# A Fourier stage: row 64 sent earlier, the last inverse matrices in two transfers, the last unit pipelined

## The chip, the cores and the metric

The kernel runs on one core of a Trainium2 chip. The metric is the device time of one execution in microseconds (us). The engines are named as in the profile: PE is the matrix engine (PEld its weight loads), DVE the vector engine, ACT the scalar engine, POOL the general engine, SP the engine that only issues transfers here.

## The reference, cut to what matters

A network of four layers over `x` (4, 96, 64, 64): a state-space layer, a depthwise convolution with a small MLP, linear attention with a quantized MLP, and a Fourier layer with a quantized MLP. The change is in the Fourier layer, which works on `t` (4 batches, 4096 tokens, 96 channels):

```python
h = jnp.einsum('bnc,hc->bnh', _ln_t(t), w1)                # 192 hidden channels
h = relu(bn1(h))
X = jnp.fft.fft(h, axis=1, norm='ortho')                   # over the 4096 tokens
xr = relu(X.real * rd - X.imag * idg + rb)
xi = relu(X.imag * rd + X.real * idg + ib)
y = jnp.fft.ifft(xr + 1j * xi, axis=1, norm='ortho').real
t = t + bn2(jnp.einsum('bnh,ch->bnc', y, w2))
```

## The kernel before

The layers run one after the other, the first to about 2610 us, the convolution to 3010, the attention with its MLP to 3319, the Fourier layer to 3863, the last MLP (`qffn`) to the end. All data of the Fourier layer stay on the chip, in `t` and `h`.

The transform of 4096 tokens is split as 128 x 32. A *unit* is half of the hidden channels (96) of one batch, so there are 8 units. A unit's forward transform goes in four *groups* of 24 of its channels (6 blocks of 4): `its` lists the 32 pairs of unit and group. One turn of the loop over `j`, called a slot below, carries several groups at different stages (matmuls are counted as the trace shows them, each of the code's fp32 ones as two):

- `over_n1(j)` (L1138): 12 matmuls with the 128-point matrix on the tile `hh`, then on DVE the twiddle products (L1142), on POOL two sums (L1150)
- `over_n2(j - 1)` (L1159 to L1162): the 32-point transform; DVE multiplies the imaginary part (L1165), ACT scales the real part in 12 instructions (L1174), POOL forms sum and difference (L1177, L1178)
- `fold(j - 2)`: ACT relu (L1184), DVE relu and add into `zz` and into `z64`, the row at frequency 64 (L1189, L1192), ACT negates one part (L1195)
- `over_k2(j - 3)` (L1207, L1208): 24 matmuls of the inverse 32-point transform, copied by ACT into the tile `bt` of the unit (L1209)
- `row64(u)` in slot 4u + 7: four small matmuls on `z64` (L1217), an ACT copy to `r` (L1219), a transfer `d<-r` to DRAM (L1221), and a transfer `bt<-d` back into row 64 of `bt` (L1222). The second waits on SP for the first
- in slots 4u + 8 to 4u + 11, two blocks a slot of the inverse 128-point transform of unit u: `over_k1` fetches four inverse matrices, 256 KB, into `gt` (L1226, two buffers), runs four matrices' matmuls on `bt` (L1229) and has ACT copy the result to `ys` (L1231). `w2` then projects (L1237), and DVE adds the result to `t` (L1241 for one half, L1243 for the other). All 32 rows `n` of `idft` take eight blocks, and every unit reads the same ones

Beside these, the next batch is normalized (`norm1`, `norm2`, L1104 to L1115) and multiplied by `w1` (L1124, L1126) in the slots of units 0 to 5, so that slots there take about 14.7 to 14.9 us, and those of units 6 and 7 about 11.6 us. After slot 31 nothing new is begun; slots 36 to 39 hold the blocks of unit 7 alone, and slots 40 to 43 are empty.

The order on PE, DVE, ACT and POOL is the order in which the code is written (`manual_schedule`). SP is not among these; the framework orders its transfers. PSUM has eight banks: two for `m` (`misc`, used by `norm1`, `norm2`, `w1`, `row64`, `over_k1` and `w2`), two for `s1`, one each for `xr` and `xi`, two for `i1` (`over_k2`). The tile `hh` has three buffers of 12 KB a partition; units 6 and 7 take the last new ones in slot 20.

Of the kernel before, what the change touches and what calls it, by code (L numbers as in the profile page):

```python
# [9 lines left out]
F32 = mybir.dt.float32  # L10
# [8 lines left out]
B, C, HW, L = 4, 96, 64, 4096  # L19
# [7 lines left out]
N1, N2, NF = 128, 32, 192  # L27
# [23 lines left out]
class Net:  # L51
# [1031 lines left out]
    def fourier(self, dram, t, h):  # L1083
        tc, nc, ins = self.tc, self.nc, self.ins
        CG, G, K1 = 24, 6, 65
        PER = CG // G
        units = [(b, half) for b in range(B) for half in range(2)]
        its = [(u, g) for u in range(len(units)) for g in range(0, CG, G)]
        with ExitStack() as ctx:
            wk = ctx.enter_context(tc.tile_pool(name="fw", bufs=1))  # L1090
            pln = ctx.enter_context(tc.tile_pool(name="fp", bufs=1, space=PSUM))
            self.tc.keep_in_program_order(nc.scalar.preload_act_table_set(ACT_EXP_LN))
            nbs, bc, bs = (self.dft2[:, k * 128 : (k + 1) * 128] for k in range(3))
            hh, bt, z64, f, x, av, zz = {}, {}, {}, {}, {}, {}, {}
            ft = [t[:, b * L : (b + 1) * L].rearrange("p (a n) -> p n a", n=N2) for b in range(B)]

            def misc(rows):
                return pln.tile([128, MB], F32, name="m_ps", tag="m", bufs=2)[:rows]
# [10 lines left out]
            def norm2(a, kept):  # L1109
                ps = misc(C)  # L1110
                nc.tensor.matmul(ps, self.ones, kept.pop(a), start=True, stop=True)
                rs = wk.tile([C, MB], F32, name="ln_rs", tag="rs")
                nc.scalar.activation(rs, ps, AF.Ln, scale=1.0 / C, bias=self.eps[:C])
                nc.scalar.activation(rs, rs, AF.Exp, scale=-0.5)
                nc.gpsimd.tensor_mul(h[:C, a : a + MB], h[:C, a : a + MB], rs)  # L1115
# [16 lines left out]
            def over_n1(i):  # L1132

                u, g = its[i]
                ps = pln.tile([128, 2, MB], F32, name="s1_ps", tag="s1")
                for d in range(G):
                    a = d % 3 * 2 * K1
                    nc.tensor.matmul(ps[:, d // 3, a : a + 2 * K1], hh[u][:, g + d], self.dft1, start=True, stop=True)  # L1138
                pp = []
                for k in range(2):  # L1140
                    p = wk.tile([128, G, 2, K1], F32, name=f"p{k}", tag=f"p{k}")
                    nc.vector.tensor_mul(  # L1142
                        p.rearrange("p (a g) r k -> p a g (r k)", a=2),
                        ps[:, :, : 6 * K1].rearrange("p a (g k) -> p a g k", g=3),
                        self.twid[:, k : k + 1, None, :].to_broadcast([128, 2, 3, 2 * K1]),
                    )
                    pp.append(p)
                f[i] = wk.tile([128, 2, G, K1], F32, name="f", tag="f", bufs=2)
                for r in range(2):
                    nc.gpsimd.tensor_add(f[i][:, r], pp[0][:, :, r, :], pp[1][:, :, 1 - r, :])  # L1150
# [46 lines left out]
            def over_k2(i):  # L1197

                u, g = its[i]
                z = zz.pop(i)  # L1200
                if g == 0:
                    bt[u] = wk.tile([N1, N2, C], F32, name="bt", tag="bt", bufs=2)
                for e in range(0, G, 3):
                    ps = pln.tile([N1, 3, 128], F32, name="i1_ps", tag="i1", bufs=2)
                    for d in range(3):
                        zd = z[:, e + d].rearrange("p k m -> p (k m)")
                        nc.tensor.matmul(ps[:, d], zd[:, 64:], bc, start=True, stop=False)  # L1207
                        nc.tensor.matmul(ps[:, d], zd[:, :128], bs, start=False, stop=True)  # L1208
                    nc.scalar.copy(  # L1209
                        bt[u].rearrange("p n (g c) -> p g n c", c=4)[:, g + e : g + e + 3],  # L1210
                        ps.rearrange("p g (n c) -> p g n c", c=4),
                    )

            def row64(u):
                ps = misc(CG)[:, :128]
                for k in range(2):
                    nc.tensor.matmul(ps, z64[u][:, k], self.dft64[:, k], start=k == 0, stop=k == 1)  # L1217
                r = wk.tile([CG, N2, 4], F32, name="r64", tag="r64", bufs=2)
                nc.scalar.copy(r, ps.rearrange("p (n c) -> p n c", c=4))  # L1219
                d = dram.tile([1, N2 * C], F32, name="d64", tag="d64", bufs=2)  # L1220
                nc.sync.dma_start(d.rearrange("o (n g c) -> g (o n) c", n=N2, c=4), r)  # L1221
                nc.sync.dma_start(bt[u][64:65].rearrange("p n c -> p (n c)"), d)  # L1222

            def over_k1(u, n, kept):
                gt = wk.tile([N1, 4, N1], F32, name="gt", tag="gt", bufs=2)
                nc.sync.dma_start(gt, ins["idft"][:, n : n + 4])  # L1226
                ps = misc(C).rearrange("p (n a) -> p n a", n=4)
                for d in range(4):
                    nc.tensor.matmul(ps[:, d], bt[u][:, n + d], gt[:, d], start=True, stop=True)  # L1229
                kept[u, n] = wk.tile([C, MB], F32, name="ys", tag="ys", bufs=2)  # L1230
                nc.scalar.copy(kept[u, n], ps.rearrange("p n a -> p (n a)"))  # L1231

            def w2(u, n, kept):

                b, half = units[u]
                ps = misc(C)
                nc.tensor.matmul(ps, self.a_w2[:, half, :], kept.pop((u, n)), start=True, stop=True)  # L1237
                ps = ps.rearrange("p (n a) -> p n a", n=4)
                td = ft[b][:, n : n + 4]
                if half == 0:  # L1240
                    nc.vector.scalar_tensor_tensor(td, ps, self.b2, td, ALU.add, ALU.add)  # L1241
                else:
                    nc.vector.tensor_add(td, td, ps)  # L1243

            engines = {mybir.EngineType.PE, mybir.EngineType.DVE, mybir.EngineType.Activation, mybir.EngineType.Pool}
            with tc.manual_schedule(engines=engines):
                for n in range(0, N2, 2):
                    w1(0, n)
                kept, sq = {}, {}
                for j in range(len(its) + 12):  # L1250
                    ub, k = divmod(j - 2 * PER, PER)
                    blocks = [(ub, n) for n in (8 * k, 8 * k + 4)] if 0 <= ub < len(units) else []

                    u, k = divmod(j, PER)
                    b = u // 2 + 1
                    normed = b < B and u % 2 == 0
                    tokens = list(range(8 * k, 8 * k + 8, 2)) if b < B and u % 2 else []
                    a = 2 * k * MB

                    def turn(count):  # L1260
                        for _ in range(min(count, len(tokens))):
                            w1(b, tokens.pop(0))

                    if j < len(its):
                        over_n1(j)

                    if normed:
                        norm1(b, a, sq)
                    if k:
                        turn(2)  # L1270
                    if 2 <= j < len(its) + 2:
                        fold(j - 2)
                    if blocks:
                        over_k1(*blocks[0], kept)
                    if normed and k:
                        norm2(a - MB, sq)
                    if 1 <= j < len(its) + 1:
                        over_n2(j - 1)
                    if normed:
                        norm1(b, a + MB, sq)  # L1280
                    if blocks:
                        w2(*blocks[0], kept)
                        over_k1(*blocks[1], kept)
                    if not k:
                        turn(2)
                    if 3 <= j < len(its) + 3:
                        over_k2(j - 3)
                    if normed:
                        norm2(a, sq)
                    if (j - 7) % PER == 0 and 0 <= (j - 7) // PER < len(units):  # L1290
                        row64((j - 7) // PER)
                    turn(len(tokens))
                    if blocks:
                        w2(*blocks[1], kept)
                    if normed and k == PER - 1:
                        norm2(a + MB, sq)


def build(tc, ins, out):
# [155 lines left out]
```

## Time and profile before

| What | us |
|---|---|
| median of three runs | 4002.08 (3991.09 to 4005.25) |
| the profiled execution | 4009.92 |
| its span | 4007.80 |
| of it the Fourier stage, 3319 to 3863 | 544 |
| PE, ACT, DVE, POOL busy in that stage | 471, 296, 242, 214 |
| the stretch of unit 7's blocks, 3836 to 3863: PE, DVE, ACT busy | 20.3, 8.8, 5.9 of 27 |

Over the whole span PE is busy 3303.4 us and DVE 3186.9, most of it in the first layer, which the change does not touch. The mean granted PE clock is 0.855 of full speed over the span, 0.94 in the Fourier stage and 0.80 in the stretch of unit 7. In the lines of a timeline the columns are the start, the length, the engine, the source line, the operation, what it writes and reads, the count, and in brackets how long the engine had been idle before and what ended that. In a window's row they are the span of time, its length, busy time and count of PE, PEld, DVE, ACT and POOL, the granted PE clock, the DMA share and GB/s.

### The profile page before, as it was taken

To read this page: it belongs to the slowest core of one execution; us is meant where nothing else is said; L and a number is where in the kernel's file an instruction comes from. 1 tells how busy PE (TensorE), PEld (TensorE's weight loads), DVE (VectorE), ACT (ScalarE), POOL (GpSimd) and SP (SyncE) were. 2 spreads that over 40 slices of the span, in tenths; PEclk is the share of its full clock that TensorE was granted. 3 is DMA by queue.
4 is the path that set the end of the run, shared out by engine and by line. 5 is a ranking of instruction groups with operands and counts; after the bars stand their busy time and mean duration, and the time that the engine had idled before them with its cause. 6 is when DMAs were issued, how large, how long until landed. Compare 5 with 4: busy or idle time off the path is not lost. (4 is left out here: it accounts for less than half of the span.)

```text
span 4007.8 us, 45514 instructions
## 1 busy us (share of the span) xinstructions
PE 3303.4 (82%) x14174; PEld 1425.1 (36%) x14174; DVE 3186.9 (80%) x2772; ACT 2421.0 (60%) x4644; POOL 2944.4 (73%) x1571
## 2 busy tenths in 40 slices
PE   6888878888888788888878888686999888998877
PEld 3222222222222222222222222186445435676642
DVE  5999999999999999999999999832652593444549
ACT  4666667667666766766666666231445575665547
POOL 2999999999999999999999999811000273444428
PEclk8888878878888888888888888667999998999989
DMA  7567566756666675666567666375000000011111
GB/s 184 137 161 174 135 160 157 175 131 168 166 154 148 162 170 138 162 166 167 141 161 169 147 155 158 82 226 178 1 0 1 1 0 6 25 35 35 42 41 54
DMA packets 183295, 468.13 MB, mean 117 GB/s; under 512 B 53240, under 2 KB 55170, under 8 KB 179972
## 3 DMA queue, kind: packets, MB, share of 16 engines
q1 hardware_dynamic: 183048, 465.21, 46.8%
q8 instruction: 113, 1.85, 0.2%
q14 instruction: 134, 1.07, 0.1%
HBM read 391.53 MB, written 73.50 MB: 116 GB/s over the span
## 5 line engine op out<-in xcount | busy, mean ns | idle before, releaser
L496 POOL TENSOR_TENSOR hs<-hs,crep 128x1024 f32<-128x1024 f32 x768 | 1796.2, 2363 | 27.2 <-DVE hs L490 22.4
L454 PE MATMUL rep<-dbl,sel_b 32*128 32x512 f32 x1152 | 409.0, 787 | 460.4 <-DVE hs L490 434.4
L474 POOL TENSOR_TENSOR up<-udb,brep 128x1024 f32<-128x1024 f32 x256 | 604.9, 2363 | 8.5 <-DMA brep<-cd 8.5
L468 ACT ACTIVATE da<-ddb,nega 128x1024 f32<-128x1024 f32 x512 | 584.9, 1149 | 14.9 <-DMA ddb<-dd 7.4
L468 ACT ACTIVATE dap<-ddb,nega 128x1024 f32<-128x1024 f32 x256 | 286.3, 1118 | 419.6 <-DVE hs L490 417.5
L515 PE MATMUL y<-hs,sel_r 128*32 128x512 f32 x3072 | 483.2, 697 | 6.1 <-POOL hs L496 6.1
L490 DVE TENSOR_TENSOR_SCAN hs<-da,state,rep 128x1024 f32<-128x1024 f32 x192 | 450.8, 2348 | 16.7
L490 DVE TENSOR_TENSOR_SCAN hs<-da,state,u 128x1024 f32<-128x1024 f32 x192 | 450.9, 2348 | 11.2 <-DVE u L486 1.4
L490 DVE TENSOR_TENSOR_SCAN hs<-dap,state,up 128x1024 f32<-128x1024 f32 x192 | 447.1, 2329 | 7.0 <-ACT dap L468 6.9
L454 PEld LDWEIGHTS rep<-dbl,sel_b 32*128 32x128 f32 x1152 | 109.6, 219 | 761.6 <-issue 510.0
L210 PE MATMUL ps<-n,w_x 97*64 97x512 f32 x1536 | 368.0, 622 | 8.1 <-ACT n L323 5.4
L486 DVE TENSOR_TENSOR u<-udb,rep 128x1024 f32<-128x1024 f32 x256 | 314.6, 1229 | 42.1 <-PE rep L454 10.9
L486 DVE TENSOR_TENSOR rep<-udb,rep 128x1024 f32<-128x1024 f32 x256 | 310.7, 1214 | 0.4
L1038 POOL CAST hq<-y 128x512 fp8e5<-128x512 f16 x192 | 118.0, 638 | 229.3 <-issue 143.0
L210 PEld LDWEIGHTS ps<-n,w_x 97*64 97x64 f32 x1536 | 109.8, 141 | 258.8 <-issue 209.2
L515 PEld LDWEIGHTS y<-hs,sel_r 128*32 128x32 f32 x3072 | 66.6, 117 | 364.5 <-issue 192.7
L382 POOL TENSOR_TENSOR du<-delta,xc 128x512 f32<-128x512 f32 x96 | 122.3, 1274 | 67.5 <-DMA gp_x<-in_x 52.1
L1177 POOL TENSOR_TENSOR av<-av,ec 128x780 f32<-128x780 f32 x32 | 58.8, 1838 | 152.3 <-ACT av L1174 152.3
L224 PE MATMUL ps<-xc,xproj 64*102 64x512 f32 x384 | 163.2, 1014 | 3.5 <-ACT xc L344 3.5
L358 ACT COPY dbl<-ps 102x512 f32<-102x512 f32 x64 | 34.3, 588 | 210.4 <-PE ps L224 210.4
L911 POOL MEMSET h<- 1x4096 f32 x1 | 3.5, 3506 | 212.9 <-DVE n L824 212.9
L490 DVE TENSOR_TENSOR_SCAN hs<-da,rep 128x1024 f32<-128x1024 f32 x64 | 146.5, 2289 | 5.4
(256 smaller groups left out, 6545.7 us busy)
## 6 DMA issues: line engine op xcount, KB each, us to landing
ddb<-dd SPq DMA_DIRECT2D x768, 128.0 KB
udb<-ud SPq DMA_DIRECT2D x768, 128.0 KB
crep<-cd SPq DMA_DIRECT2D x512, 128.0 KB
brep<-cd SPq DMA_DIRECT2D x256, 128.0 KB
dd<-delta SPq DMA_DIRECT2D x64, 384.0 KB
ud<-du SPq DMA_DIRECT2D x192, 128.0 KB
band<-in_band SPq DMA_DIRECT2D x24, 1024.0 KB
gt<-in_idft SPq DMA_DIRECT2D x64, 256.0 KB
```

The costliest lines, as they stand in the source:

```text
L210: nc.tensor.matmul(ps[rows], w[:, 64 * p : 64 * p + 64], rhs[:, at.start + shift : at.stop + shift], start=k == 0, stop=k == len(ws) - 1, ...
L224: nc.tensor.matmul(ps, w[rows, p], x[rows, p], start=start and p == 0, stop=p == 2)
L382: nc.gpsimd.tensor_mul(u, m["delta"][:, of], m["xc"][:, of])
L454: nc.tensor.matmul(x[:, at], sel_b[rows, order[t][1]], made[k]["dbl"][rows, at], start=True, stop=True)
L468: nc.scalar.activation(da, made[k]["dd", h, j], AF.Exp, scale=nega[:, col : col + 1])
L474: nc.gpsimd.tensor_mul(u, made[k]["ud", h, j], made[k]["brep", g])
L486: nc.vector.tensor_mul(u, made[k]["ud", h, j], x)
L490: nc.vector.tensor_tensor_scan(hs[:, 1:], made[k].pop(("da", t)), u, 0.0 if s == 0 else st, ALU.mult, ALU.add)
L496: nc.gpsimd.tensor_mul(hs[:, :T], hs[:, 1:], made[k]["crep", order[t][1]])
L515: nc.tensor.matmul(made[k]["y", p][row : row + 32], sel_r, made[k]["hs", t][:, at], start=False, stop=True, skip_group_check=True,)
L1038: nc.gpsimd.tensor_copy(q[:, m, :], y2, saturate=False)
L1177: nc.gpsimd.tensor_add(v[:, 2:4], v[:, 0:2], ec)
```

## The change

Four things change, all in `fourier`.

- `fetch(k)` loads half of `idft` (16 of 32 matrices, 1 MB) into a free buffer of the tag `hh`, in slots 25 and 29. From then on `over_k1` takes its matrices from there if it finds its `n` in `late`, and else fetches `gt` as before. So `gt` is still used by units 0 to 3 and in six blocks of unit 4.
- The loop ends after slot 35. Unit 7's eight blocks follow in a loop of their own, in which `over_k1` of a block is issued ahead of `w2` of the block before.
- `w2` of unit 7 writes to the two banks of `i1` in place of `m`; for that the tile of `i1` becomes 4 x 128 wide, of which `over_k2` uses three quarters.
- `row64(u)` is issued in slot 4u + 6 in place of 4u + 7.

```diff
@@ over_k2
-                    ps = pln.tile([N1, 3, 128], F32, name="i1_ps", tag="i1", bufs=2)
+                    ps = pln.tile([N1, 4, 128], F32, name="i1_ps", tag="i1", bufs=2)[:, :3]
@@ ahead of over_k1
+            late = {}
+
+            def fetch(k):
+
+                g = wk.tile([N1, CG, N2, 4], F32, name="hh", tag="hh", bufs=3)
+                g = g.rearrange("p g n c -> p (g n c)")[:, : N2 // 2 * N1].rearrange("p (n a) -> p n a", n=N2 // 2)
+                nc.sync.dma_start(g, ins["idft"][:, k * N2 // 2 : (k + 1) * N2 // 2])
+                for n in range(0, N2 // 2, 4):
+                    late[k * N2 // 2 + n] = g[:, n : n + 4]
+
             def over_k1(u, n, kept):
-                gt = wk.tile([N1, 4, N1], F32, name="gt", tag="gt", bufs=2)
-                nc.sync.dma_start(gt, ins["idft"][:, n : n + 4])
+                if n in late:
+                    gt = late[n]
+                else:
+                    gt = wk.tile([N1, 4, N1], F32, name="gt", tag="gt", bufs=2)
+                    nc.sync.dma_start(gt, ins["idft"][:, n : n + 4])
@@ w2
-                ps = misc(C)
+                if u < len(units) - 1:
+                    ps = misc(C)
+                else:
+                    ps = pln.tile([N1, 4, 128], F32, name="i1_ps", tag="i1", bufs=2)[:C].rearrange("p n a -> p (n a)")
@@ the loop over slots
-                for j in range(len(its) + 12):
+                for j in range(len(its) + 4):
...
                     if j < len(its):
                         over_n1(j)
+                    if j in (len(its) - 7, len(its) - 3):
+                        fetch((j - len(its) + 7) // 4)
...
-                    if (j - 7) % PER == 0 and 0 <= (j - 7) // PER < len(units):
-                        row64((j - 7) // PER)
+                    if (j - 6) % PER == 0 and 0 <= (j - 6) // PER < len(units):
+                        row64((j - 6) // PER)
...
+                last = [(len(units) - 1, n) for n in range(0, N2, 4)]
+                for k, block in enumerate(last):
+                    over_k1(*block, kept)
+                    if k:
+                        w2(*last[k - 1], kept)
+                w2(*last[-1], kept)
```

## The prediction

> **What bounds the kernel now.** The page first: VectorE is busy 80% and TensorE 82% of the span, but by stages. The windows view of 3319 to 3863 us, the Fourier stage, gives PE 471 of 544 us, ACT 296, DVE 242, POOL 214: PE leads there, and short holes in PE are what an edit can win. So I read the waits of 3420 to 3862 next ("who <- whom: us in total, times, longest"):
>
> ```profile
> PE m_ps L1237 <- ACT ys L1231: 23.3, 23, 4.5
> PE m_ps L1229 <- DMA bt<-d: 16.6, 5, 5.6
> PE m_ps L1229 <- issue: 8.3, 2, 4.8
> SPq L1222 <- DMA d<-r: 25.2, 8, 3.8
> ```
>
> Together 24.9 us of PE stood before the first `over_k1` of seven units, waiting for row 64; no line names PE waiting for `gt<-in_idft`. Then the timeline (start, length, engine, line; in brackets the idle time before) at one unit's boundary, SP, PE and ACT:
>
> ```profile
> 3786.49 0.33 SPq L1221 DMA_DIRECT2D d<-r  x1
> 3788.31 0.85 ACT L1184 ACTIVATE av<-av 128x780 f32<-128x780 f32 x1 [1.84 <-POOL av L1178]
> 3790.33 0.52 ACT L1195 ACTIVATE zz<-zz 128x384 f32<-128x384 f32 x1 [1.17 <-DVE zz L1189]
> 3790.66 0.24 SPq L1222 DMA_DIRECT2D bt<-d  x1
> 3792.79 1.99 PE L1229 MATMUL m_ps<-gt,bt 128*96 128x128 f32 x8 [5.58 <-DMA bt<-d]
> 3794.82 0.58 ACT L1231 COPY ys<-m_ps 96x512 f32<-96x512 f32 x1 [3.96 <-PE m_ps L1229]
> 3799.51 3.66 ACT L1174 ACTIVATE av<-xr_ps,vec 128x65 f32<-128x65 f32 x12 [4.11 <-PE xr_ps L1162]
> ```
>
> The reader is to see the trip of row 64 through DRAM (6.3 us from L1221 to L1229), and two ACT waits behind it, 3.96 and 4.11: the second, before the long L1174, is the delay that the slot passes on. And the eight L1229 matmuls take 1.99 us, against 1.04 elsewhere. Last, the tail, where unit 7 runs alone, and the clock there:
>
> ```profile
> 3836.02 1.99 PE L1229 MATMUL m_ps<-gt,bt 128*96 128x128 f32 x8 [4.83 <-issue]
> ...
> 3850.26 1.10 PE L1237 MATMUL m_ps<-ys,a_w2s 96*96 96x512 f32 x2 [0.72 <-ACT ys L1231]
> 3851.19 1.04 PE L1229 MATMUL m_ps<-gt,bt 128*96 128x128 f32 x8
> 3852.95 1.10 PE L1237 MATMUL m_ps<-ys,a_w2s 96*96 96x512 f32 x2 [0.72 <-ACT ys L1231]
> ```
>
> ```profile
> 3836.00:3840.00 4.00, 3.25 (x10) 2.34 (x11) 0.00 (x0) 0.58 (x1) 0.00 (x0) 0.50 0.16 60
> 3840.00:3844.00 4.00, 3.27 (x10) 1.96 (x9) 1.14 (x1) 0.58 (x1) 0.00 (x0) 0.50 0.12 30
> ```
>
> One block every 2.70 us, of which PE waits 0.72 for the ACT copy (the column after POOL is the granted clock: 0.50 for the first 8 us after the 4.83 us hole).
>
> **The change, part by part.** "Slot" is a turn j of the loop; times are of the trace before.
>
> *Row 64 a slot ahead.* Four matmuls (0.62 us), the copy L1219 (0.25), and two SP issues (0.33 and 0.24, with SP held between them 25.2/8 = 3.2 us) go from slot 4u+7 to 4u+6, past one slot's work on PE, ACT and SP; nothing of it is on POOL or DVE. Work is neither added nor saved. The data then have a slot (11.6 us at the least) more for a trip that needs 5.7 to 6.3 us, so the holes close. What is late next is the ACT order: L1174 follows `ys` (0.58), which follows L1195, which follows the fold on DVE, and these do not depend on row 64; PE also has to finish L1162. The gain per boundary is the start of L1174 now, less the later of (end of L1195 + 0.6) and L1162's end at full clock:
> - unit 1: 3504.01 now; 3499.60 + 0.6 = 3500.2: 3.8
> - unit 2: L1195 ends 3568.14, `ys` and L1174 follow without a gap: 0 (the 1.46 us hole is covered)
> - unit 3: 3632.56; 3627.84 + 0.6 = 3628.4: 4.2
> - unit 4: 3695.28; 3693.52 + 0.6 = 3694.1: 1.2
> - unit 5: 3746.51; 3741.51 + 0.6 = 3742.1: 4.4
> - unit 6: 3799.51; 3790.85 + 0.6 = 3791.4 (PE, started at 3787.4, is through xr at 3791.4 too): 8.1
> - unit 7: the first L1229 starts at 3836.02; row 64 would be issued at 3825.5, land at 3825.5 + 3.1 + 2.4 = 3831.0, and PE, with 0.6 more in slot 34, gets there at 3831.4: 4.6
> - unit 0: PE has no hole: 0
>
> Sum 26.3. Here a rule weighs in: the Trainium skill (TensorE: Matmul & The Clock Gate, Part 1: The HAM clock gate) says that TensorE falls to half clock after an idle window of about 3.4 us and is let go after about 3.4 us of sustained work. By it each of the four holes over 3.4 us (units 3, 5, 6, 7) costs its length plus 1.7, and all seven holes give 24.95 + 6.8 = 31.8. The rows differ both ways: after 5.58 us the slow time lasted to about 3798.5, after 4.83 us to about 3847, and at units 1 to 4 other engines cover part of the hole. I take the rows: 26.3.
>
> In slot 4u+6 the row takes one of the two `m` banks, so the next `w2` or `w1` on PE waits for the ACT copy L1219. In slot 4u+7 of before such waits were 1.5, 1.3, 1.1 (PEld and PE <- ACT r). They move along; 0, with ±1 us a unit as bounds, since the two slots hold the same kinds of work.
>
> On SP, `gt` of the next unit, released by `over_k1` early in slot 4u+7, may stand behind `bt<-d` by some 2 us (slot 27: `gt` at 3725.9 now, `bt<-d` would go at about 3723.7 + 3.8 = 3727.5). It has a slot to arrive and needs 2.3 us (issue to last packet): 0. If SP's order put the pair ahead of both `gt` of slot 4u+7, these would land some 6 us into that slot and be wanted 1.5 to 3.3 us in; SP's order is not written by hand, so this is a rival.
>
> *Two fetches.* Two of 1 MB replace 26 of the 64 `gt` transfers. No row has 1 MB in this stage; the nearest is `band<-in_band`, 13 issues of 1 MB in 43.53 us, so some 3.6 us each and 4.5 for a lone one. The first waits on SP for the last reader of the third `hh` buffer, `over_n1(23)` (ends 3674), and is wanted at 3702; the second waits for `over_n1(27)` (3725), wanted at 3765. Behind them on SP stand `bt<-d` of units 4 and 5 and the `gt` of unit 4; at 6 us late these still have 5 us or more in hand. Cost 0 (bounds 0 and 7: one such hole with its slow clock). Gain in the loop 0, since nobody waits for `gt` there; in the tail it keeps the transfer (2.3 us, two buffers) off a block of under 2 us.
>
> *Four banks in the tail.* `over_k1` of the next block now runs while ACT copies the last one, and `w2` has banks of its own. A block then costs PE its two starts: L1237 to L1229 0.94 (3850.26 to 3851.19) and eight L1229 0.89, 1.83 us; ACT (0.58) and DVE (1.15) fit below. Eight blocks and the last copy: 8 x 1.83 + 0.72 + 0.16 = 15.5, against 3836.02 to 3862.15 = 26.1: 10.6. Two statements of that page speak against it: in HAM oscillation, a kernel in which PSUM double-buffering gave no further gain, and in its second failure mode, that cycling through banks with micro-idles lets the clock swing. At half clock a block costs 1.81 (3838.74 to 3840.55) and 1.8, eight 29.0, and the edit loses about 4. I hold to the rows: with the fetched halves in SBUF PE has no hole in the tail before its last copy, and 2.70 us blocks with a hole each ran at full clock from 3847 on. The four empty turns dropped and the wider `i1` tile (same two banks) cost nothing.
>
> Sum: 26.3 + 10.6 = 36.9 us. The profiled execution took 4009.92 (span 4007.80 and 2.1 around it), giving 3973.0; the median of the three runs is 4002.08, 7.8 lower, so 3965.
>
> **The rivals.**
> 1. *The clock carries over.* The next stage begins at clock 0.50 (3866 to 3878); a dense tail may leave it full there. Four ramp steps at 4.41 us now (L887 to L887) would be about 2.8: 6.5 more, 3958. Against: its own holes of 0.7 and 1.25.
> 2. *`gt` late instead.* SP's order as above. Rows 1 to 5 would each move a hole of some 3.5 us to slot 4u+7; units 6 and 7 have no `gt` and keep their gain: 36.9 - 17.5 = 19.4, so 3983. Against: before, SP had issued both `gt` of the next unit ahead of `d<-r` at every unit.
> 3. *The tail stays at half clock.* 36.9 - 10.6 - 4 = 22: 3980.
> 4. *Slower: row 64's bank.* In slot 4u+6 the matmul behind the row waits for L1219, which stands on ACT behind L1174 (3.66) and `ys`. If ACT is late there, each slot loses up to 5 us; eight make 40, and the time is 4005. It decides above 36.9/8 = 4.6 us a unit; the longest such wait now is 1.5.
> 5. *Nothing moves* (the holes only follow the longest chain): 4002.
>
> **How the numbers follow.** The main case has 0.60 (3955 to 3976), rival 1 0.12, rival 2 0.10, rival 3 0.10, rival 4 0.05, rival 5 0.03. Half a per cent, about what a measurement of this kernel can tell from no change, is 20 us: rival 2 lies on that edge and is halved. Faster 0.60 + 0.12 + 0.10 + 0.05 = 0.87, same 0.05 + 0.03 = 0.08, slower 0.05. The range, 3950 to 3984, takes in rivals 1 to 3 and the fetch's bound of 7.
>
> **What would show it.** The line "PE m_ps L1229 <- DMA bt<-d" gone; slots 12, 20, 28 near 18.4, 16.8 and 11.4 us instead of 22.2, 21.0 and 15.8; the L1237 and L1229 starts of the tail 1.83 apart in pairs, at full clock, over 15.5 us; two 1 MB issues of `idft`. Wrong would be: PE waiting for `gt<-in_idft`, or for L1219 over 4 us; tail blocks of 3.6 us; a fetch landing after its first `over_k1` was due.

## The result, and the profile after

The changed kernel takes 3970.63 us, the median of five runs (3969.60 to 3976.28), against 4002.08 for five of the kernel before. The ratio is 0.9926, 95% interval 0.9913 to 0.9938: 25 to 35 us faster. A second set of five, on another occasion, gave 3976.14 and 0.9933 (0.9919 to 0.9947). The profiled execution took 3970.14, span 3968.40; it had been 4009.92 and 4007.80. So the first two profiles lie 39.4 apart and the medians about 31; second profiles of both kernels, below, show why.

First the waits of the changed kernel, 3420 to 3830 us (L1229 is now L1242, L1237 is L1253, the copy to `ys` L1244; `m_ps<-hh,bt` is `over_k1` with fetched matrices), and those of SP:

```profile
PE m_ps L1253 <- ACT ys L1244: 29.7, 23, 4.0
SPq L1222 <- DMA d<-r: 20.9, 8, 3.4
SPq L1230 <- PE s_ps L1138: 1.7, 1, 1.7
```

The line in which PE waited for `bt<-d` is gone, and L1242 has no other long wait in its place. But about half of those 24.9 us came back one step later. Before, `w2` waited 23.3 us for the copy `ys`, 5.8 of it in the eight blocks of unit 7; outside unit 7 that wait has grown from 17.5 to 29.7 us. The largest new ones are 3.06 us each, in slots 12 and 20, behind the fold. SP still stands between the two transfers (20.9 us in eight), but nobody waits for it. SP's wait for `hh`, the only one the fetches caused, came to 1.7 us, once. Next the timeline at the boundary to unit 6, SP, ACT and PE:

```profile
3761.90 0.33 SPq L1221 DMA_DIRECT2D d<-r  x1
3765.08 0.21 SPq L1222 DMA_DIRECT2D bt<-d  x1
3774.03 1.04 PE L1242 MATMUL m_ps<-hh,bt 128*96 128x128 f32 x8
3778.06 0.52 ACT L1195 ACTIVATE zz<-zz 128x384 f32<-128x384 f32 x1 [1.17 <-DVE zz L1189]
3778.49 0.56 ACT L1244 COPY ys<-m_ps 96x512 f32<-96x512 f32 x1
3778.96 3.63 ACT L1174 ACTIVATE av<-xr_ps,vec 128x65 f32<-128x65 f32 x12
```

Row 64 leaves 12.1 us before it is wanted. The matmuls start at once and at full clock (1.04 for 1.99), `ys` and L1174 follow L1195 without a gap: the 3.96 and 4.11 us waits are both gone. Last the tail, PE in the middle of unit 7, and the window of the whole stretch:

```profile
3815.38 1.04 PE L1242 MATMUL m_ps<-hh,bt 128*96 128x128 f32 x8
3816.25 1.02 PE L1253 MATMUL i_ps<-ys,a_w2s 96*96 96x512 f32 x2
3817.11 1.04 PE L1242 MATMUL m_ps<-hh,bt 128*96 128x128 f32 x8
```

```profile
3810.40:3825.20 14.80, 14.40 (x81) 9.39 (x80) 9.07 (x8) 5.81 (x9) 0.00 (x0) 1.00 0.01 1
```

A block starts every 1.73 us, no bracket here shows a wait (the only one in unit 7 is 0.38 us, at its second block), and PE is busy 14.40 of 14.80 us at clock 1.00.

### The profile page after: what moved, and what is told of

Its sections match the earlier page's. It is cut to its first block, busy times and chain, and to the rows that moved or that the text cites. A ratio compares the mean times of both kernels' runs of the same rounds, so it can differ in the third digit from the quotient of the medians.

```text
span 3968.4 us, 45450 instructions
## 1 busy us (share of the span) xinstructions
PE 3256.8 (82%) x14174; PEld 1408.1 (35%) x14174; DVE 3182.4 (80%) x2772; ACT 2419.8 (61%) x4644; POOL 2943.4 (74%) x1571
## 5 line engine op out<-in xcount | busy, mean ns | idle before, releaser
L454 PE MATMUL rep<-dbl,sel_b 32*128 32x512 f32 x1152 | 398.6, 768 | 484.2 <-DVE hs L490 449.0
L382 POOL TENSOR_TENSOR du<-delta,xc 128x512 f32<-128x512 f32 x96 | 123.9, 1291 | 65.4 <-DMA gp_x<-in_x 49.1
L224 PE MATMUL ps<-xc,xproj 64*102 64x512 f32 x384 | 146.6, 920 | 3.5 <-ACT xc L344 3.5
L490 DVE TENSOR_TENSOR_SCAN hs<-da,u 128x1024 f32<-128x1024 f32 x64 | 146.5, 2288 | 3.7 <-DVE u L486 0.5
```

What stands on the lines that cost most here:

```text
L224: nc.tensor.matmul(ps, w[rows, p], x[rows, p], start=start and p == 0, stop=p == 2)
L382: nc.gpsimd.tensor_mul(u, m["delta"][:, of], m["xc"][:, of])
L454: nc.tensor.matmul(x[:, at], sel_b[rows, order[t][1]], made[k]["dbl"][rows, at], start=True, stop=True)
L490: nc.vector.tensor_tensor_scan(hs[:, 1:], made[k].pop(("da", t)), u, 0.0 if s == 0 else st, ALU.mult, ALU.add)
```

## Experiments

Times below are medians of several runs where no other count is given; each ratio is to the kernel before, run beside it on the same chip. Stretches are read from the one profile of each run.

**Row 64 alone.** The one line of the loop, and nothing else:

```diff
-                    if (j - 7) % PER == 0 and 0 <= (j - 7) // PER < len(units):
-                        row64((j - 7) // PER)
+                    if (j - 6) % PER == 0 and 0 <= (j - 6) // PER < len(units):
+                        row64((j - 6) // PER)
```

> Row 64 issued a slot ahead, nothing else changed. Theory (row 64's trip through DRAM is the larger part): the holes before the first over_k1 of a unit close, slots 12, 20 and 28 shorten by 2 to 4 us, unit 7 starts 13 us sooner after slot 31, and its blocks run at full clock from the start (8 x 2.70 = 21.6 us in place of 26.1). 20 to 29 us faster, ratio 0.993 to 0.995. Rival (the tail's banks are the larger part): under 12 us faster, ratio above 0.997.

Measured 3983.63, ratio 0.9950 (0.9938 to 0.9963): the upper edge of the ratio that the theory named (18.8 us by the medians, just short of its 20), and not the rival's. From the start of slot 31 to unit 7's start it took 47.9 us, as in the full change (61.3 before). The tail's blocks stay serial, and PE waits for the copy in each, but at full clock from the first:

```profile
3813.52 1.08 PE L1229 MATMUL m_ps<-gt,bt 128*96 128x128 f32 x8 [0.41 <-DMA bt<-d]
3815.33 1.10 PE L1237 MATMUL m_ps<-ys,a_w2s 96*96 96x512 f32 x2 [0.73 <-ACT ys L1231]
3816.26 1.04 PE L1229 MATMUL m_ps<-gt,bt 128*96 128x128 f32 x8
```

Unit 7 takes 21.8 us here, 4.3 less than before, so that much of the old tail was slow clock behind the hole.

**The tail alone, with `gt`.** Row 64 in its old slot, no `fetch`:

```diff
-                    if j in (len(its) - 7, len(its) - 3):
-                        fetch((j - len(its) + 7) // 4)
...
-                    if (j - 6) % PER == 0 and 0 <= (j - 6) // PER < len(units):
-                        row64((j - 6) // PER)
+                    if (j - 7) % PER == 0 and 0 <= (j - 7) // PER < len(units):
+                        row64((j - 7) // PER)
```

> Only the tail over four banks; row 64 as before, matrices still through gt. Theory (the tail is bound by PE's starts, the transfer of 256 KB with two buffers just keeps pace): blocks 1.8 to 1.9 us apart at full clock, but the hole before unit 7 stays (4.8 us) with slow blocks of 3.6 us behind it; tail 16 to 21 us, 5 to 10 us faster, ratio 0.9975 to 0.9988. Rival (the fetch is needed for the tail): PE waits for gt<-in_idft in the tail, blocks of 2.5 us or more, no gain.

Measured 3993.82, ratio 0.9975 (0.9966 to 0.9985), and 18.35 us for unit 7. The theory held in size, but the rival had a part: PE does meet the transfer, twice.

```profile
3836.62 1.08 PE L1242 MATMUL m_ps<-gt,bt 128*96 128x128 f32 x8 [0.35 <-DMA gt<-in_idft]
...
3841.18 1.08 PE L1242 MATMUL m_ps<-gt,bt 128*96 128x128 f32 x8 [0.87 <-DMA gt<-in_idft]
```

After these come blocks 1.9 to 2.1 us apart where fetched halves allow 1.74.

**The fetches alone.** The kernel before with `late`, `fetch` and the test in `over_k1`; loop, tail and row 64 as they were:

```diff
+                    if j in (len(its) - 7, len(its) - 3):
+                        fetch((j - len(its) + 7) // 4)
```

> Only the two fetches of 1 MB; loop, tail and row 64 as before. Theory: nobody waited for gt, so no change, within 2 us, ratio 0.9995 to 1.0005, holes of row 64 as before. Rival (the gt transfers held up row 64's pair on SP or in the queues): the trip in units 5 to 7 gets shorter by 1 us or more each and the time falls by 4 to 8 us.

Measured 4001.19, ratio 0.9995 (0.9987 to 1.0003): no change, with PE's wait for row 64 still there.

```profile
PE m_ps L1242 <- DMA bt<-d: 19.7, 6, 5.1
```

**The whole change without row 64's lead.** Slot 4u + 7 again, the fetches and the tail kept:

```diff
-                    if (j - 6) % PER == 0 and 0 <= (j - 6) // PER < len(units):
-                        row64((j - 6) // PER)
+                    if (j - 7) % PER == 0 and 0 <= (j - 7) // PER < len(units):
+                        row64((j - 7) // PER)
```

> The whole change with row 64 put back in slot 4u + 7. Theory: what is left is the tail's gain, less the slow clock behind the hole before unit 7: tail 16 to 21 us, 5 to 10 us faster, ratio 0.9975 to 0.9988, like the tail alone without fetch. Rival (the parts do not add: without row 64's lead the tail gains nothing, since the slow clock takes it): under 3 us.

Measured 3990.37, ratio 0.9966 (0.9952 to 0.9979), a little more than the range named, and clearly not the rival's. Unit 7 takes 15.8 us, with the hole of 4.97 in front of it:

```profile
3827.53 3.55 PE L1242 MATMUL m_ps<-hh,bt 128*96 128x128 f32 x16 [4.97 <-DMA bt<-d]
```

Against the tail with `gt` it is 2.6 us shorter in the stretch of unit 7: the fetches' worth, and only there. In its profile, which was its fastest execution (3984.17), the next stage began at full clock, and the *ramp*, from the end of unit 7 to the first `h_ps` of the last MLP, took 11.0 us, where the changed kernel's took 15.4. Whether that also lifted the median above the range named is not shown (more on the ramp below).

**The changed kernel again, and two banks.** The first is the same kernel, for a second profile. In the other, unit 7's `w2` takes the `m` banks:

```diff
-                if u < len(units) - 1:
-                    ps = misc(C)
-                else:
-                    ps = pln.tile([N1, 4, 128], F32, name="i1_ps", tag="i1", bufs=2)[:C].rearrange("p n a -> p (n a)")
+                ps = misc(C)
```

> The changed kernel once more, beside the variants below and as a second profile of it. Theory: the same stages as in its first profile: slots 12 and 20 at 20.1 and 18.5 us, unit 7's stretch 14.8 us, ratio to before 0.992 to 0.994. The clock at the start of the next stage is the open point: if the free choice of the clock window decides, the ramp there (tail's end to the first h_ps) is 11 us in some profiles and 15 in others of the same kernel.

> The whole change, but unit 7's w2 takes the two m banks that over_k1 uses, as everywhere else; the order stays pipelined. Theory (the extra banks matter): w2 must wait for the DVE add of the w2 before (1.15 us), blocks about 2.2 us apart, unit 7's stretch 17 to 19 us, 2 to 4 us slower than the changed kernel. Rival (the order alone does it): blocks 1.74 us apart as with four banks, no difference.

The second profile of the changed kernel repeats slots 12 and 20 (20.1 and 18.5) and unit 7 (14.8). Its ramp was the long one again. But from slot 0 to unit 7's end it took 494.0 us, the first 490.3; the difference lies in slots 5 to 8, 52.8 us at a granted clock of 0.90 in place of 49.1 at 1.00. With two banks the median is 3978.84, ratio 0.9944 (0.9932 to 0.9957), against 3976.14 and 0.9933 (0.9919 to 0.9947) beside it: the intervals overlap, so the whole time can't decide 2.7 us, but the stretch does. Unit 7 takes 18.2 us, 2.34 a block, and the hole is the DVE add's:

```profile
3824.64 1.10 PE L1250 MATMUL m_ps<-ys,a_w2s 96*96 96x512 f32 x2 [0.36 <-DVE t L1256]
3825.58 1.04 PE L1242 MATMUL m_ps<-hh,bt 128*96 128x128 f32 x8
3826.98 1.10 PE L1250 MATMUL m_ps<-ys,a_w2s 96*96 96x512 f32 x2 [0.37 <-DVE t L1256]
```

So with row 64's lead unit 7 takes 21.8 us serially, 18.2 with the order and the fetches over two banks, and 14.8 over four. Three were not tried.

**POOL's sums moved to DVE, in two slots.** For the two slots in which the gain fell short:

```diff
-                    nc.gpsimd.tensor_add(f[i][:, r], pp[0][:, :, r, :], pp[1][:, :, 1 - r, :])
+                    (nc.vector if i in (12, 20) else nc.gpsimd).tensor_add(f[i][:, r], pp[0][:, :, r, :], pp[1][:, :, 1 - r, :])
```

> The changed kernel with the two sums L1150 of slots 12 and 20 on DVE in place of POOL. Theory (in these slots the fold's L1189 runs beside POOL's sums and takes 2.73 us for 0.55, which is why they fell by 2 us and not by 4): L1189 takes 0.55 there and L1195 follows; the two sums cost DVE 1 to 2 us, so the slots change little. Rival (L1189 waits for something else, so its length has nothing to do with POOL): L1189 is as long as before in both slots.

One run, 3969.04. In slot 12 the changed kernel has on DVE and POOL:

```profile
3494.53 2.73 DVE L1189 SCALAR_TENSOR_TENSOR zz<-av 128x384 f32<-128x384 f32 x1 [0.26 <-ACT av L1184]
...
3493.76 1.27 POOL L1115 TENSOR_TENSOR h<-h,ln_rs 96x512 f32<-96x512 f32 x1 [1.46 <-ACT ln_rs L1114]
3494.99 1.85 POOL L1150 TENSOR_TENSOR f<-p,p 128x390 f32<-128x390 f32 x2
```

and with the sums on DVE:

```profile
3493.90 1.62 DVE L1150 TENSOR_TENSOR f<-p,p 128x390 f32<-128x390 f32 x2
3495.44 0.54 DVE L1189 SCALAR_TENSOR_TENSOR zz<-av 128x384 f32<-128x384 f32 x1
```

L1189 ends 0.4 us after POOL's second sum in the first, and takes 0.54 for 2.73 in the second, where POOL is idle beside it (its product L1115 ends at 3494.63). That its length comes from POOL's work beside it is shown, in slot 20 as well (2.73 and 0.54). It agrees with the Trainium skill (SBUF — State Buffer, Who interferes with whom): a DVE instruction with two SBUF inputs contends with a GpSimd instruction that reads SBUF.

The sums then cost DVE 1.62 us ahead of the fold, so what is won is less: L1195 starts 6.15 us into the slot in place of 7.02, 0.9 us sooner. The theory had the slots change little. Slot 12 took 17.6 us (20.1 in the changed kernel) and slot 20 took 19.4 (18.5), but the granted clock differed: 1.00 against 0.92 in slot 12, 0.82 against 1.00 in slot 20. Slots at the same clock are compared further on, under "Both together".

**The last slots reordered.** What was left before unit 7 was a PE hole of 4 us behind the last fold (the 4.0 in the first wait line above). After slot 32 the loop is replaced by:

```diff
-                for j in range(len(its) + 4):
+                for j in range(len(its) + 1):
...
+                v = len(units) - 2
+                over_k1(v, 8, kept)
+                over_k1(v, 12, kept)
+                fold(len(its) - 1)
+                over_k2(len(its) - 2)
+                w2(v, 8, kept)
+                over_k2(len(its) - 1)
+                row64(v + 1)
+                w2(v, 12, kept)
-                last = [(len(units) - 1, n) for n in range(0, N2, 4)]
+                last = [(v, n) for n in range(16, N2, 4)] + [(v + 1, n) for n in range(0, N2, 4)]
```

with `w2` on the `i1` banks for those twelve blocks.

> The changed kernel with its last slots reordered: after slot 32 unit 6's two next blocks and the copies of their results go ahead of the last fold, the last two over_k2 and row 64 follow at once, and the other twelve blocks of units 6 and 7 run in one pipeline over four banks. Theory (what is left before unit 7 is a hole of 4 us behind the fold, its slow clock, and six unit-6 blocks at 2.7 us or more): unit 7 ends about 9 us sooner, ratio to before near 0.990. Rival (row 64's trip of 6 us is the bound again, since it now starts with fewer blocks in hand): a hole of 2 us or more before unit 7 and a gain of less than 5 us over the changed kernel.

Measured 3964.99, ratio 0.9909 (0.9895 to 0.9922), 11 us below the changed kernel beside it. From the start of slot 31 to unit 7's end it takes 54.2 us (62.7 in the changed kernel), and there is no hole before unit 7. The theory's 9 us is met: 8.5 in the stretch.

**Both together, and a filled hole.** The reordered kernel with the two slots' sums on DVE; and that with two matmuls behind the last `w2`:

```diff
                 w2(*last[-1], kept)
+                ps = pln.tile([128, 2, MB], F32, name="s1_ps", tag="s1")
+                for d in range(2):
+                    nc.tensor.matmul(ps[:C, d], self.ones, h[:C, :MB], start=True, stop=True)
```

> The reordered kernel with the sums L1150 of slots 12 and 20 on DVE as well. Theory (the two gains lie in different slots and add): slots 12 and 20 at 17.6 and 17 to 19 us in place of 20.1, unit 7's end as in the reordered kernel, 3 to 5 us faster than that, ratio to before near 0.9895. Rival (the next slots give it back): same as the reordered kernel within 1 us.

> The kernel e9_order_sums with two matmuls more on PE behind the last w2, into a bank that nobody reads: they fill PE's hole of 1.2 us at the start of the next stage. Theory (one window of 3.4 us that holds this hole and the one of 0.78 after it drops the clock to a half for four windows): the clock stays full, the ramp from unit 7's end to the first h_ps takes about 11 us in place of 15, 3 to 5 us faster than e9_order_sums. Rival (the clock falls by the low load of the ramp itself, whatever goes before): the ramp stays at 15 us or more and the two matmuls cost up to 1 us.

The first: 3959.49, ratio 0.9899 (0.9880 to 0.9917); slots 12 and 20 took 19.2 and 17.6 us (20.2 and 20.1 in the reordered kernel). Not all of that is the sums' doing. Slot 20 in the changed kernel, the reordered one, this one, and the one with the sums on DVE alone:

```profile
3616.80:3635.26 18.46, 14.54 (x81) 11.62 (x80) 7.59 (x9) 10.11 (x28) 8.24 (x7) 1.00 0.10 29
3620.10:3640.18 20.08, 16.16 (x81) 13.24 (x80) 7.57 (x9) 10.12 (x28) 8.23 (x7) 0.92 0.09 27
3616.39:3633.99 17.60, 14.54 (x81) 11.62 (x80) 6.99 (x11) 10.12 (x28) 6.43 (x5) 1.00 0.10 31
3614.00:3633.38 19.38, 17.06 (x81) 13.78 (x80) 6.93 (x11) 10.22 (x28) 6.42 (x5) 0.82 0.09 28
```

The first two run the same code up to there, and differ by 1.6 us with the clock. At clock 1.00 the sums on DVE make 17.6 of 18.5; in slot 12, at 0.91 and 0.92, they make 19.2 of the changed kernel's 20.1. So the move is worth 0.9 us in each slot, 1.8 in both. The median lies 5.5 us under the reordered kernel's, but the intervals overlap, and 1.8 of it is what has a shown cause. The second: 3958.46, 0.9892 (0.9877 to 0.9907), the same within the noise. The clock stayed full in the ramp of both profiles, so the filling tells nothing: whether it could hold the clock stays open.

**The kernel before, a second profile.**

> The kernel before once more, for a second profile of it. Theory: the first profile was a slow draw (4009.92 against a median of 4002), so the stretch from slot 0 to unit 7's end is shorter here by some us than the 526.2 of the first profile, and the difference of the two profiles shown (39 us) is larger than that of the medians for this reason. Rival: that stretch repeats within 1 us, and the surplus lay in other stages.

One run, 4000.10, span 3998.0: from slot 0 to unit 7's end 521.9 us in place of 526.2, as the theory had it, but the larger part of the surplus lies after it. The windows from unit 7's end to the first `h_ps` of the next stage, the first profile, then the second:

```profile
3862.10:3878.30 16.20, 12.81 (x16) 3.27 (x16) 2.53 (x3) 5.91 (x10) 0.00 (x0) 0.55 0.00 1
```

```profile
3858.10:3869.00 10.90, 6.91 (x16) 2.14 (x16) 2.38 (x3) 5.08 (x10) 0.00 (x0) 1.00 0.00 1
```

The stretch with the same 16 matmuls takes 16.2 us at clock 0.55, or 10.9 at 1.00. So one kernel shows both, and 5.4 of the 9.8 us between the two profiles of before is this. It is not what set the first pair of profiles 39 us apart, since both had the long ramp (16.2 and 15.4). There the stretch from slot 0 to unit 7's end made 35.9 of the 39.4: a slow draw of before (526.2, then 521.9) met a quick one of the changed kernel (490.3, then 494.0). The means of two profiles each, 524.0 and 492.1, lie 31.9 apart, as the medians do.

## Why the prediction was right, point by point

Forecast 3965, range 3950 to 3984; measured 3970.6. The mechanism of each part was met. The sizes (start of L1138 to start of L1138 for a slot; the last column is the mean of two profiles of each kernel):

| Term | predicted, us | first profiles | mean of two |
|---|---|---|---|
| unit 0, slots 5 to 8 | 0 | 51.4 to 49.1: 2.3 | 0.0 |
| unit 1, slot 12 | 3.8 | 22.2 to 20.1: 2.1 | 2.2 |
| unit 3, slot 20 | 4.2 | 21.0 to 18.5: 2.5 | 2.4 |
| unit 4, slot 24 | 1.2 | 12.6 to 11.6: 1.0 | 0.8 |
| unit 5, slot 28 | 4.4 | 15.8 to 11.6: 4.2 | 4.3 |
| units 6 and 7, slot 31's start to unit 7 | 8.1 + 4.6 | 61.3 to 47.9: 13.4 | 12.5 |
| tail | 10.6 | 26.1 to 14.8: 11.3 | 10.4 |
| sum without unit 0 | 36.9 | 34.5 | 32.6 |
| slot 0 to unit 7's end | | 526.2 to 490.3: 35.9 | 31.9 |

- *Row 64's step*: right; alone it gave ratio 0.9950. The mis-sized terms are those of units 1 and 3, 3.4 us short together. The step that failed there is "these do not depend on row 64": L1195 was taken to end where it had ended. In the kernel before, slot 12 starts at 3493.90, in the changed one at 3490.82; ACT in the one, then in the other:

```profile
3495.78 0.84 ACT L1184 ACTIVATE av<-av 128x780 f32<-128x780 f32 x1
3499.08 0.52 ACT L1195 ACTIVATE zz<-zz 128x384 f32<-128x384 f32 x1 [2.45 <-DVE zz L1189]
3493.59 0.84 ACT L1184 ACTIVATE av<-av 128x780 f32<-128x780 f32 x1
3497.84 0.52 ACT L1195 ACTIVATE zz<-zz 128x384 f32<-128x384 f32 x1 [3.42 <-DVE zz L1189]
```

L1195 starts 7.0 us into the slot for 5.2, and L1174 7.9 us where the sum had 6.3. Half of these 1.8 us is DVE's fold, which moved against POOL's norm product and sums (L1189 2.73 us); moving the sums gave 0.9 back. The other half comes ahead of the fold: the relu L1184 starts 2.8 us into the slot for 1.9. That agrees in size with the 0.9 us by which slot 11 got shorter, so PE is sooner there and ACT's norm work ahead of the relu is not; no run separates this.
- *The neighbours' bank*: slots 10, 14, 18 and 22 grew by 0.7 to 1.4 us and slots 11, 15, 19 and 23 shrank by 0.7 to 0.9, so each pair nets 0 to 0.5: within the ±1 given. Rival 4's 4.6 us a unit never came near.
- *SP's order*: the framework put `bt<-d` ahead of the next unit's `gt` as reckoned, and the fetches two slots early, in 23 and 27 (at 3669.95 and 3716.96); PE met no transfer in the loop. Rival 2 is refuted.
- *Fetches*: 0 in the loop, shown; 2.6 us in the tail (18.35 against 15.8 for unit 7), a gain to which the prediction gave no size of its own.
- *Four banks*: 1.83 predicted a block, 1.74 measured. The kernel to which double-buffering gave nothing, on the page that the prediction cites, was no guide here: two banks cost 18.2, four 14.8. Nor did the cycling through banks bring the clock down, which was 1.00 in the tail (rival 3).
- *The clock*: for row 64's holes the estimate by that page's rule was 31.8 and that by the rows 26.3; measured are 34.5 - 11.3 = 23.2 by the first profiles and 22.2 by the means, so the rows were nearer. Other engines cover part of a hole, as the waits for `ys` show. Rival 1 (the next stage keeps full clock) did not happen in either profile of the changed kernel (the ramp took 15.4 and 15.6 us), yet it did in the second profile of before and in four of the variants.
- *The sum against a median*: the forecast was 5.6 us too low. By the means of two profiles the terms came to 32.6, which is 4.3 below the forecast, and 3.4 of that is units 1 and 3. The first profiles alone hide it: in the second one of before the stretch from slot 31 to unit 7 took 59.5 us (61.3 in the first) and the tail 24.3 (26.1), so 3.6 us of the gain seen there was the draw. The prediction had treated the first profile's 7.8 us above the median as neutral.

## What to carry to other kernels

A trip through DRAM that must come back before a step wants a whole slot of lead, and moving four matmuls, one copy and two issues one slot earlier can be free even on a busy engine. When a hole closes, ask what is late next and what it now runs beside: here about half of PE's wait came back as a wait for the next copy, and a DVE instruction that met POOL's reads cost 0.9 us in each of two slots. Compare two profiles of each kernel before a term is read to the microsecond: slots with the same code differed by 1.6 us with the clock alone. Serial pairs of matmul, copy and matmul at the end of a stage should be pipelined over as many banks as the add behind them needs.

## What the runs showed of the hardware that was not expected

The half clock comes in steps. In the clock records of all these profiles a stretch at half clock, in the Fourier stage and the ramp, lasts 3.41 us or a whole multiple of it: in the changed kernel 3.41 in slot 12, 6.83 at the 4 us hole ahead of unit 7, 13.65 in the ramp. The 3.4 us just ahead of that last one, and the stretch itself:

```profile
3824.90:3828.30 3.40, 1.41 (x4) 0.30 (x3) 1.44 (x2) 1.02 (x2) 0.00 (x0) 1.00 0.00 0
3828.30:3842.00 13.70, 12.34 (x16) 3.64 (x17) 1.49 (x3) 6.34 (x11) 0.00 (x0) 0.50 0.00 1
```

So the clock fell behind 3.4 us in which PE was busy for 1.41 and its two holes were only 1.21 and 0.78 us long. And at half clock a PE that is 90% busy by the profile was not let go for 13.65 us, which is more than the 3.4 us of sustained work that the Trainium skill names (TensorE: Matmul & The Clock Gate, Part 1). The same stretch ran at full clock in other executions, behind the same work. Where the step's window falls was not steered by any run here, and how busy PE must be to keep or regain the full clock stays open.
